# Graph attention with gathered neighbours: the norm constants made for four tiles at once, the output stores spaced, and four operations moved between engines

## The chip, the cores and the metric

The kernel runs on one core of a Trainium2 chip. A core has five engines that work side by side, each through its own list of instructions in order: TensorE (PE in the profile: matmuls; PEld is its loading of weights), VectorE (DVE), ScalarE (ACT), GpSimd (POOL) and SyncE (SP, which only starts DMA transfers here). An engine whose next instruction has to wait stands still, even if a later one could run. The metric is the time of one execution on the device in microseconds, the median of several runs. The profile is of one further execution.

## The reference

Sixteen graphs of 1024 nodes with 512 features share one adjacency matrix. Layer norm and a rectifier, projections to queries, keys and values with 8 heads of 64, softmax over the neighbours of each node, a weighted sum of their values, and x added at the end:

```python
h = jnp.maximum(_layernorm(x, axis=-1), 0.0)
q = (h @ Wq + bq).reshape(b, n, H, HD)      # k and v alike
scores = jnp.einsum('bihd,bjhd->bhij', q, k) / jnp.sqrt(jnp.float32(HD))
mask = jnp.where(adj == 0, jnp.float32(-1000000000.0), jnp.float32(0.0))
weights = jax.nn.softmax(scores + mask[None, None, :, :], axis=-1)
out = jnp.einsum('bhij,bjhd->bihd', weights, v)
x = x + out.reshape(b, n, H * HD)
```

The adjacency matrix is sparse: an entry is one with a probability that falls with the node's number, 1/256 on average, and the diagonal is one.

## The kernel before

The kernel sorts the nodes by degree, so that a tile of 128 nodes has rows of like length, and makes a list of each node's neighbours. That is the preparation, once for all graphs. For each graph it then loads x in sorted order, normalizes it, makes keys and values, stores them in DRAM, and gathers for every node the keys and values of its neighbours, one neighbour ("slot") of 128 nodes per indirect transfer. A tile has 2 to 11 slots, taken in "units" of at most four; the rows that are longer than 11 have the rest in unit 11 ("pieces"):

```python
CAPS = (11, 8, 6, 5, 4, 3, 3, 2)      # slots of tiles 0 to 7
UNITS = (                              # (tile, first slot, slots); the tile -1 is that of the pieces
    (7, 0, 2), (6, 0, 3), (5, 0, 3), (4, 0, 4), (3, 0, 3), (3, 3, 2), (2, 0, 3),
    (2, 3, 3), (1, 0, 4), (1, 4, 4), (0, 0, 4), (-1, 0, 4), (0, 4, 4), (0, 8, 3),
)                                      # units 0 to 13
POOL_FOLDS = (2, 3, 8, 9, 10, 11, 12)
BY_VECTOR = {2: 1, 3: 0, 4: 1}         # slots of a unit that VectorE weighs; ScalarE weighs the others
POOLS = dict(x=14, h=2, pht=2, hT=11, pkv=2, kvt=3, q=2, q0=1, g=6, acc=2, o=1)   # buffers
```

The order of every engine's instructions is worked out while the kernel is built. A plan lists the operations with an engine, a length, a place (the smaller, the earlier it is preferred), what they follow and which buffers they use; it then lets the five engines run on paper and notes what starts when. The kernel is emitted in just that order:

```python
add(("stats", n), "DVE", 0.90, p - ahead - 3.82, [("load_x", n)], [("x", n)])
if b and n % 2:
    add(("variance", n // 2), "DVE", 0.33, ..., [("stats", n - 1), ("stats", n)])
    add(("power", n // 2), "POOL", 0.82, ..., [("variance", n // 2)])
    add(("shift", n // 2), "DVE", 0.23, ..., [("power", n // 2)])
add(("norm", n), "ACT", 0.81, p - 6.37, [("shift", n // 2) if b else ("load_x", n)], [("x", n), ("h", n)], delay=0.09)
add(("flip", n), "PE", 0.62, p - 3.76, [("norm", n)], [("h", n), ("pht", n)])
add(("unflip", n), "ACT", 0.58, p - 1.28, [("flip", n)], [("pht", n), ("hT", n)])
# [...] proj_kv, evict_kv, store_kv (keys and values), queries (pq), gathers
add(("multiply", k), "DVE", 0.15 + 0.533 * count, i, slots + [q_of[q]], [g, q])
add(("score", k), "DVE", 0.15 + 0.533 * count, i - -0.31, [("multiply", k)], [g])
# [...] exponent, row_sums, share, weigh_v, weigh_s, fold, join, add_up, scale
add(("residual", b, home), "POOL", 1.42, i + 2.49, [("scale", b, home)], [o, ("x", n)])
add(("put_out", b, home), "POOL", 1.5, i + 0.07, [("residual", b, home)], [("x", n)], delay=4.0, moves=0.75)
```

What the operations do, as far as they matter here (cut):

```python
def stats(n):                                   # VectorE: mean and variance of a tile
    m, k = divmod(n, 2)
    nc.vector.bn_stats(st, X[n]); nc.vector.bn_aggr(MV[m][:, k, :], st)
def variance(m): nc.vector.tensor_scalar_add(RSTD[m], MV[m][:, :, 1], EPS)
def power(m):    nc.gpsimd.tensor_tensor(RSTD[m], RSTD[m], minus_half.to_broadcast([P, 2]), ALU.pow)
def shift(m):    nc.vector.scalar_tensor_tensor(SHIFT[m], MV.pop(m)[:, :, 0], -1.0, RSTD[m], op0=ALU.mult, op1=ALU.mult)
def norm(n):     nc.scalar.activation(HN[n], X[n], AF.Relu, bias=shift, scale=scale)
def flip(n):     # TensorE: four transposes of h into pht; unflip copies pht to hT on ScalarE
def multiply(i): nc.vector.tensor_tensor(k, k, Q[b, t][:, None, :].to_broadcast([P, count, D]), ALU.mult)   # gathered keys by pq
def score(i):    nc.vector.tensor_reduce(weights[:, w, :], heads(G[i][:, :count, 0, :]), AX.X, ALU.add)
def weigh_v(i):  # VectorE: the last n slots' values by their weights, one instruction
    n = by_vector(b, B, count)
def weigh_s(i, s):                              # ScalarE: one slot, one instruction per head
    for h in range(H):
        nc.scalar.activation(v[:, h, :], v[:, h, :], AF.Identity, scale=weights[:, c + s, h : h + 1])
def fold(i, first, n):                          # adds slots first to first+n on to slots 0 to n
    engine = nc.gpsimd if n == 1 and i % NU in POOL_FOLDS else nc.vector
    engine.tensor_tensor(v[:, 0:n], v[:, 0:n], v[:, first : first + n], ALU.add)
def residual(b, t):                             # x + attention
    (nc.vector if shares_in(b, B, t) and b == B - 1 else nc.gpsimd).tensor_tensor(rows, rows, add, ALU.add)
def put_out(b, t):                              # stores the rows at their nodes' places
    nc.gpsimd.indirect_dma_start(out=out_rows, out_offset=on(ap=perm[:, t : t + 1], axis=0), in_=..., in_offset=None, element_offset=b * N * D)
```

Units of four slots are folded twice: slots 2 and 3 on to 0 and 1 (VectorE), then 1 on to 0 (VectorE or, in the units of POOL_FOLDS, GpSimd). The sum of tile 0 over its units, with the pieces among them, is made on TensorE (add_up, into acc); those of the other tiles on VectorE (join). The last graph is taken in another order, with more of the sums on TensorE.

Of the kernel before, what the change touches and what calls it, by code (L numbers as in the profile page):

```python
# [32 lines left out]
P = 128  # L33
# [33 lines left out]
POOL_FOLDS = (2, 3, 8, 9, 10, 11, 12)  # L67
# [4 lines left out]
BY_VECTOR = {2: 1, 3: 0, 4: 1}  # L72
BY_VECTOR_LAST = {2: 1, 3: 1, 4: 2}
POOLS = dict(x=14, h=2, pht=2, hT=11, pkv=2, kvt=3, q=2, q0=1, g=6, acc=2, o=1)
# [95 lines left out]
def plan_of(B):  # L170
# [30 lines left out]
    for what, known, made in (("key", [("keys",)], -52.56), ("rank", [("ranks",)], -49.22)):  # L201
        for half in range(2):
            row = ("q", what, half)
            add(("flip_row", what, half), "PE", 0.6, made, known, [row])
            add(("copy_row", what, half), ("DVE", "ACT")[half], 0.65, made, [("flip_row", what, half)], [row, sources])
    rows = lambda what: [("copy_row", what, half) for half in range(2)]
    for t in range(NT):
        add(("rank_of", t), ("DVE", "ACT")[t >= NT // 2], 1.25, (-47.51, -44.58)[t >= NT // 2], rows("key"))
    add(("ranks",), "DVE", 1.4, -47, [("rank_of", t) for t in range(NT)])
    add(("ends",), "DVE", 0.7, -45, rows("rank"), [sources])  # L210
    for t in range(NT):
        add(("list_of", t), "DVE", 2.5, -35.55 + t, [("ends",), ("no_diagonal", t)], [sources])
        behind = lambda name: [(name, t - 2)] if t > 1 else [("zeros",)]
        add(("tell", t), "POOL", 1.3, -35.76 + 0.3 * t, [("ranks",), ("shift", (t - NT) // 2)] + behind("tell"), delay=2.0)
        add(("spread", t), "POOL", 1.3, -28.64 + t, [("list_of", t)] + behind("spread"), delay=2.0)
    add(("collect", "told"), "SP", 0.05, -39, [("tell", t) for t in range(NT)], delay=2.6)
    add(("collect", "lists"), "SP", 0.05, -31, [("spread", t) for t in range(NT)], delay=2.6)
    add(("others",), "DVE", 1.3, -34.38, [("ends",)], [sources])
    add(("perm_of",), "DVE", 0.5, -31, [("collect", "told")])
    add(("spots",), "DVE", 3.9, -38.36, [("collect", "lists")])  # L220
    add(("long_rows",), "POOL", 1.3, -39.76, [("perm_of",)], [("g", -2)], 2.5, 1.5)
    add(("long_blocks", 0), "DVE", 1.25, -18.02, [("long_rows",), ("others",)], [sources, ("g", -2)])
    for k in range(1, 5):
        add(("long_blocks", k), "DVE", 2.0, -32.13 + 0.1 * k, [("long_blocks", k - 1)], [("g", -2)])
# [4 lines left out]
    add(("count_pieces",), "DVE", 0.9, 2.64, [("longest", ROUNDS - 1)])  # L229
# [6 lines left out]
    add(("slots", 0), "DVE", 2.0, 3.84, [("pieces",), ("spots",)])  # L236

    for n in range(-NT, tiles):
        b, j = divmod(n, NT)
        ahead = 0 if n >= 0 else 11.19 - 1.3 * j  # L240
        p = (b - 1) * NU + j * rate if b > 0 else j * rate - 19.58 if b == 0 else 1.5 * j - 44.63
        if n >= 0:
            known = [("perm_of",)] if b == 0 else []
            add(("load_x", n), "POOL", 1.40, p - 7.17, known, [("x", n)], delay=4.5, moves=0.75)
        if b:
            add(("stats", n), "DVE", 0.90, p - ahead - 3.82, [("load_x", n)], [("x", n)])
        if b and n % 2:
            add(("variance", n // 2), "DVE", 0.33, p - ahead - 5.75, [("stats", n - 1), ("stats", n)])
            add(("power", n // 2), "POOL", 0.82, p - ahead - 4.87, [("variance", n // 2)])
            add(("shift", n // 2), "DVE", 0.23, p - ahead - 4.31, [("power", n // 2)])  # L250
        add(("norm", n), "ACT", 0.81, p - 6.37, [("shift", n // 2) if b else ("load_x", n)], [("x", n), ("h", n)], delay=0.09)
        add(("flip", n), "PE", 0.62, p - 3.76, [("norm", n)], [("h", n), ("pht", n)])
        add(("unflip", n), "ACT", 0.58, p - 1.28, [("flip", n)], [("pht", n), ("hT", n)])
        if b == 0:
            continue
        for w in range(2):
            e = p - 0.39 + 0.3 * w
            ready = [("unflip", n)]
            if n < 0:
                ready += [("round", "kv"[w], 2), ("load_w", "kv"[w])]  # L260
            add(("proj_kv", n, w), "PE", 3.70, e, ready, [("hT", n), ("pkv", n, w)])
            add(("evict_kv", n, w), "ACT", 0.58, e - 0.43, [("proj_kv", n, w)], [("pkv", n, w), ("kvt", n)])
        ready = [("evict_kv", n, w) for w in range(2)]
        if n >= 0:
            add(("store_kv", n), "SP", 0.1, p, ready, [("kvt", n)], delay=2.5, moves=1.5)
        else:
            add(("store_kv", n), "POOL", 1.35, p, ready + [("ranks",)] + ([("store_kv", n - 1)] if n > -NT else []), [("kvt", n)], delay=2.5, moves=1.5)

    q_of = {}
    for k in range(units):  # L270
        b, u = divmod(k, NU)
        i = b * NU + (LAST_ORDER.index(u) if b == B - 1 else u)
# [3 lines left out]
        if q not in q_of:  # L276
            p = i - 2.15
            if t >= 0:
                ready = [("unflip", n)] + ([("round", "q", 2), ("load_w", "q")] if b == 0 else [])
                add(("queries", b, t), "PE", 3.66, p, ready, [("hT", n), q])  # L280
                if t == 0:
                    add(("copy_q", b), "ACT", 0.57, p + 0.5, [("queries", b, 0)], [q, ("q0", b)])
            else:
                add(("queries", b, t), "PE", 0.9, p, [("copy_q", b)], [q, ("q0", b)])
            q_of[q] = ("queries", b, t)
# [3 lines left out]
        for s, slot in enumerate(slots):  # L289
            if is_own(u, s):  # L290
                add(slot, "SP", 0.1, i - -0.51, stored if b == 0 else [("store_kv", n)], [g], delay=2.5, moves=1.5)
                continue
            add(slot, "POOL", 1.35, i - 4.33 + 0.1 * s, stored, [g], delay=4.0, moves=1.5)
        vector = by_vector(b, B, count)
        add(("multiply", k), "DVE", 0.15 + 0.533 * count, i, slots + [q_of[q]], [g, q])
        add(("score", k), "DVE", 0.15 + 0.533 * count, i - -0.31, [("multiply", k)], [g])
        shares = shares_in(b, B, t)
        add(("exponent", k), "ACT", 0.22, i + -0.73, [("score", k)], delay=0.60)
        weights = ("exponent", k)
        if shares:  # L300
            weights = ("share", k)
            add(("row_sums", b, t), "DVE", 0.47, i + 0.98, [("exponent", k)])
            add(weights, "DVE", 0.3, i + -1.42, [("row_sums", b, t)])
        weighed = []
        if vector:
            weighed.append(("weigh_v", k))
            add(("weigh_v", k), "DVE", 0.15 + 0.533 * vector, i + 1.76, [weights], [g])
        for s in range(count - vector):
            weighed.append(("weigh_s", k, s))
            add(("weigh_s", k, s), "ACT", 1.97, i + 0.86 + 0.1 * s, [weights], [g], delay=0.20)  # L310
        for n in folds(b, B, t, count):
            on_pool = n[1] == 1 and u in POOL_FOLDS
            add(("fold", k, *n), "POOL" if on_pool else "DVE", 1.38 if on_pool else 0.84 * n[1] - 0.15, i + 0.78, weighed, [g], delay=1.79 if on_pool else 0.15)
# [4 lines left out]
        if without_tensor(b, B, home):  # L318
            acc = ("g", b * NU + parts[0])
            added = weighed  # L320
            if u != parts[0]:
                added = [("join", k)]
                add(("join", k), "DVE", 0.84, i + 2.33, weighed + summed, [g, acc])
            summed = added
        else:
            add(("add_up", k), "PE", 0.88 * (1 if folds(b, B, t, count) else count), i + 0.84, weighed + ([("add_up", k - 1)] if u != parts[0] else []), [g, acc])
            added = [("add_up", b * NU + v) for v in parts]
        if u == parts[-1]:
            n = b * NT + NT - 1 - home
            if shares:  # L330
                add(("residual", b, home), "POOL" if b < B - 1 else "DVE", 1.42, i + 5.31, weighed, [g, ("x", n)])
                add(("put_out", b, home), "POOL", 1.5, i + 2.40, [("residual", b, home)], [("x", n)], delay=4.0, moves=0.75)
                continue
# [3 lines left out]
            if home == 0:  # L337
                pieces = [b * NU + v for v in parts if UNITS[v][0] < 0]
                add(("more", b), "DVE", 0.22, pieces[0] + 1.35, [("exponent", v) for v in pieces])
                add(("pass_on", b), "PE", 0.3, pieces[0] + 0.69, [("more", b)], [("acc", b, "more")])  # L340
                exps.append(("pass_on", b))
            add(sums, "DVE", 0.47 if home else 0.72, i + 1.79, exps, [] if home else [("acc", b, "more")])
            add(("scale", b, home), "DVE", 0.85, i + 0.78, [sums] + added, [acc, o])
            add(("residual", b, home), "POOL", 1.42, i + 2.49, [("scale", b, home)], [o, ("x", n)])
            add(("put_out", b, home), "POOL", 1.5, i + 0.07, [("residual", b, home)], [("x", n)], delay=4.0, moves=0.75)
    return plan.ordered(POOLS)

# [16 lines left out]
def by_vector(b, B, count):  # L364

    return (BY_VECTOR if b < B - 1 else BY_VECTOR_LAST)[count]

# [14 lines left out]
def main_path(tc, x, adj, Wq, bq, Wk, bk, Wv, bv, out, sums, cover):  # L382
# [10 lines left out]
    with ExitStack() as ctx:  # L393
# [200 lines left out]
        def stats(n):  # L594
            m, k = divmod(n, 2)
            st = small.tile([P, nc.vector.BN_STATS_DIM], F32, tag="st", name=f"st_{n}")
            if m not in MV:
                MV[m] = small.tile([P, 2, nc.vector.BN_AGGR_DIM], F32, tag="mv", name=f"mv_{m}")
# [3 lines left out]
        def made(m, at, name):  # L602
            t = 2 * m + NT
            return before["told"][:, t : t + 2, at] if m < 0 else small.tile([P, 2], F32, tag=name, name=f"{name}_{m}")
# [5 lines left out]
        def power(m):  # L610
            nc.gpsimd.tensor_tensor(RSTD[m], RSTD[m], minus_half.to_broadcast([P, 2]), ALU.pow)
# [5 lines left out]
        def norm(n):  # L617
            b, t = tile_at(n)
            m, k = divmod(n, 2)
# [271 lines left out]
        def weigh_v(i):  # L891
            b, t, w, c, count = unit(i)
            n = by_vector(b, B, count)
# [69 lines left out]
        def residual(b, t):  # L963
            rows = X[b * NT + NT - 1 - t]
            add = G.pop(b * NU + parts_of(t)[0])[:, 0, 1, :] if shares_in(b, B, t) else O.pop((b, t))
            (nc.vector if shares_in(b, B, t) and b == B - 1 else nc.gpsimd).tensor_tensor(rows, rows, add, ALU.add)  # L966
# [202 lines left out]
```

## Time and profile before

| | |
|---|---|
| median of 3 runs | 1759.28 us (1757.06 to 1759.89) |
| span of the profiled execution | 1752.1 us |
| TensorE, VectorE, ScalarE, GpSimd busy | 1618.9, 1558.5, 1489.1, 1330.9 us |
| TensorE clock granted, mean | 0.97 |
| moved by DMA | 531.73 MB, 303 GB/s |
| indirect gathers / loads of x / output stores on GpSimd | 608 / 128 / 128 |
| shift, 60 of 128x2 | 52.6 us, 877 ns each |
| power, 60 of 128x2 | 60.6 us, 1010 ns each |
| folds of 128x512: GpSimd / VectorE | 120 of 1279 ns / 181 of 823 ns |
| residuals on GpSimd | 127 of 1268 to 1288 ns |
| weighing of 128x512 on VectorE | 128 of 828 ns |

A line of the profile that tells of waits reads: who waited, at which line of the kernel, for whom; then the total in us, how often, and the longest. A line of the timeline reads: start, length, engine, line, operation, what is written from what, and in brackets how long the engine stood before it, and what released it. GpSimd's transfers are told as DMA_INDIRECT: the time is that in which GpSimd writes their descriptors, not that of the transfer.

### The profile page before, as it was taken

How to read it: one execution, taken by the hardware profiler on the slowest of the kernel's cores; microseconds unless marked ns; L12 is line 12 of the kernel's file. 1: busy time of each engine (PE TensorE's matmuls, PEld its weight loads, DVE VectorE, ACT ScalarE, POOL GpSimd, SP SyncE). 2: the span in 40 equal slices, each digit the busy share in tenths (PEclk: the TensorE clock that was granted, in tenths of full speed). 3: DMA queues.
4: the chain of work that ended last, by engine and by line, in shares of the span. 5: the costliest groups of instructions: out<-in, count | busy, mean ns of one | idle time of the engine just before them, and what ended most of it. 6: DMA issues, size and time to landing. Idle time of an engine off the chain costs nothing.

```text
span 1752.1 us, 19712 instructions
## 1 busy us (share of the span) xinstructions
PE 1618.9 (92%) x4295; PEld 751.8 (43%) x4295; DVE 1558.5 (89%) x1922; ACT 1489.1 (85%) x5556; POOL 1330.9 (76%) x1235
## 2 busy tenths in 40 slices
PE   6979898999999999999999999999999999999796
PEld 3444444444444444444444444444444444444333
DVE  5788989899898979989898998989989898988897
ACT  5359989898898988889898888989899898889965
POOL 4757778787787868877787877878787787877774
PEclk9989999999999999999999999999999999999989
DMA  5388889888898988988898888989988898888894
GB/s 219 132 321 293 309 292 344 309 324 316 287 329 304 339 298 309 323 284 327 305 350 303 304 304 293 346 318 328 322 294 313 293 346 304 318 311 290 310 359 169
DMA packets 150742, 531.73 MB, mean 303 GB/s; under 512 B 19916, under 2 KB 19916, under 8 KB 150616
## 3 DMA queue, kind: packets, MB, share of 16 engines
q0 software_dynamic: 109840, 390.70, 62.5%
q1 hardware_dynamic: 40776, 139.71, 21.7%
q8 instruction: 36, 0.59, 0.1%
q14 instruction: 90, 0.74, 0.1%
HBM read 429.51 MB, written 100.82 MB: 303 GB/s over the span
## 4 chain that ended last, share of the span: by engine, by line
PE 45%; DVE 18%; POOL 8%; ACT 6%; issue 4%; DMA 3%; POOLq 0%; DVEq 0%
PE pq L642 15%; PE pk L642 12%; PE pv L642 8%; DVE g L876 5%; ACT g L902 4%; PE acc L925 4%; DVE g L907 3%; DVE weights L880 3%; PE pht L632 3%; POOL g L866 3%; DVE shift L615 3%; DMA out_dram<-x,perm 2%; POOL x L966 2%; POOL g L907 1%; DVE g L896 1%
## 5 line engine op out<-in xcount | busy, mean ns | idle before, releaser
L902 ACT ACTIVATE g<-g,weights 128x64 f32<-128x64 f32 x4768 | 1180.3, 340 | 3.2 <-DVE weights L889 2.2
L866 POOL DMA_INDIRECT g<-kv,index x608 | 626.1, 1030 | 204.6 <-issue 143.5
L876 DVE TENSOR_TENSOR g<-g,pq 128x1536 f32<-128x1536 f32 (+2 forms) x208 | 389.1, 1872 | 95.4 <-PE pq L642 90.9
L642 PE MATMUL pq<-wq,hT 128*128 128x512 f32 x1024 | 460.3, 592 | 0.0
L642 PE MATMUL pk<-wk,hT 128*128 128x512 f32 x960 | 439.0, 601 | 1.8 <-ACT hT L637 1.7
L642 PE MATMUL pv<-wv,hT 128*128 128x512 f32 x960 | 431.6, 592 | 0.0
L880 DVE TENSOR_REDUCE weights<-g 128x32 f32<-128x2048 f32 (+2 forms) x224 | 423.2, 1890 | 0.6
L907 DVE TENSOR_TENSOR g<-g 128x512 f32<-128x512 f32 (+1 forms) x271 | 281.1, 1038 | 21.9 <-ACT g L902 19.8
L642 PEld LDWEIGHTS pq<-wq,hT 128*128 128x128 f32 x1024 | 194.7, 190 | 228.0 <-issue 224.7
L642 PEld LDWEIGHTS pk<-wk,hT 128*128 128x128 f32 x960 | 185.8, 194 | 212.9 <-issue 206.0
L642 PEld LDWEIGHTS pv<-wv,hT 128*128 128x128 f32 x960 | 182.5, 190 | 205.3 <-issue 201.9
L969 POOL DMA_INDIRECT out_dram<-x,perm x128 | 148.1, 1157 | 79.2 <-DMA out_dram<-x,perm 34.2
L625 ACT ACTIVATE h<-x,shift,rstd 128x512 f32<-128x512 f32 x120 | 91.3, 809 | 91.5 <-DVE shift L615 91.5
L590 POOL DMA_INDIRECT x<-in_x_dram,perm x128 | 135.9, 1062 | 34.9 <-issue 32.4
L907 POOL TENSOR_TENSOR g<-g 128x512 f32<-128x512 f32 x120 | 153.5, 1279 | 10.7 <-DVE g L907 7.2
L632 PE MATMUL pht<-ident,h 128*128 128x128 f32 x512 | 86.2, 308 | 80.2 <-ACT h L625 78.2
L632 PEld LDWEIGHTS pht<-ident,h 128*128 128x128 f32 x512 | 68.3, 158 | 139.5 <-ACT h L625 104.5
L896 DVE TENSOR_TENSOR g<-g,weights 128x512 f32<-128x512 f32 (+1 forms) x134 | 114.5, 855 | 2.2 <-ACT weights L884 1.7
L653 ACT COPY kvt<-pv 128x512 f32<-128x512 f32 x120 | 69.2, 577 | 43.0 <-PE pv L642 43.0
L966 POOL TENSOR_TENSOR x<-x,o 128x512 f32<-128x512 f32 x67 | 86.3, 1288 | 25.0 <-DVE o L957 22.1
L925 PE MATMUL acc<-g,ident 128*128 128x512 f32 x170 | 95.6, 682 | 2.8 <-POOL g L907 2.8
L637 ACT COPY hT<-pht 128x512 f32<-128x512 f32 x128 | 72.1, 575 | 26.9 <-PE pht L632 26.9
(231 smaller groups left out, 1187.0 us busy)
## 6 DMA issues: line engine op xcount, KB each, us to landing
g<-kv SPq DMA_DIRECT2D x128, 512.0 KB
kv<-kvt SPq DMA_DIRECT2D x120, 512.0 KB
g<-kv,index POOLq DMA_INDIRECT x608, 7.2
adj<-in_adj_dram SPq DMA_DIRECT2D x8, 512.0 KB
x_first<-in_x_dram SPq DMA_DIRECT2D x8, 256.0 KB
x<-in_x_dram,perm POOLq DMA_INDIRECT x128, 4.6
out_dram<-x,perm POOLq DMA_INDIRECT x128, 5.0
wk<-in_L_gnn_Wk_dram SPq DMA_DIRECT2D x1, 1024.0 KB
```

The costliest lines, as they stand in the source:

```text
L590: nc.gpsimd.indirect_dma_start(out=X[n][:], out_offset=None, in_=x_rows, in_offset=on(ap=perm[:, t : t + 1], axis=0), element_offset=b * N * D
L632: nc.tensor.transpose(PH[n][:, c, :], hn[:, ts(c, P)], ident)
L642: nc.tensor.matmul(pt, HT[n][:, c, :], W[name][:, c, :], start=False, stop=(c == DC - 1))
L866: nc.gpsimd.indirect_dma_start(out=G[i][:, s].rearrange("p j d -> p (j d)"), out_offset=None, in_=KV[b % len(KV)][:], in_offset=on(ap=inde ...
L876: nc.vector.tensor_tensor(k, k, Q[b, t][:, None, :].to_broadcast([P, count, D]), ALU.mult)
L880: nc.vector.tensor_reduce(weights[:, w, :], heads(G[i][:, :count, 0, :]), AX.X, ALU.add)
L896: nc.vector.tensor_tensor(v, v, own.to_broadcast([P, n, H, HD]), ALU.mult)
L902: nc.scalar.activation(v[:, h, :], v[:, h, :], AF.Identity, scale=weights[:, c + s, h : h + 1])
L907: engine.tensor_tensor(v[:, 0:n], v[:, 0:n], v[:, first : first + n], ALU.add)
L925: nc.tensor.matmul(ACC[b, home], owner_t if t < 0 else ident, v[:, s, :], start=(u == parts_of(home)[0] and s == 0), stop=(u == parts_of(h ...
L966: (nc.vector if shares_in(b, B, t) and b == B - 1 else nc.gpsimd).tensor_tensor(rows, rows, add, ALU.add)
L969: nc.gpsimd.indirect_dma_start(out=out_rows, out_offset=on(ap=perm[:, t : t + 1], axis=0), in_=X.pop(b * NT + NT - 1 - t)[:], in_offset=No ...
```

## The change

Four parts, and an order that is worked out anew:

- The norm's constants (variance, power, shift) are made for four tiles in one instruction each, not for two. The tiles of the first pass (which prepares the first graph) stay in pairs.
- Each output store follows, in the plan, the landing of the one before it. The stores write to one DRAM tensor at places known only at run time, so the kernel waits for that in any case; now the plan knows of it and can put other work between.
- Two of GpSimd's folds (units 10 and 12) and the sum with x of tile 4 go to VectorE; in the last graph, tile 7's sum with x goes from VectorE to GpSimd.
- VectorE weighs one slot of unit 6, which ScalarE did.

Beside these, lengths and places in the plan are set anew. All this is for taking load off GpSimd and ScalarE and for fewer hand-overs between engines ahead of the normalization. Nothing is computed differently.

```diff
-POOL_FOLDS = (2, 3, 8, 9, 10, 11, 12)
+POOL_FOLDS = (2, 3, 8, 9, 11)
+ONE_MORE = (6,)
+VECTOR_RESIDUAL = (4,)
 [...]  places and lengths of the preparation
-        if b and n % 2:
-            add(("variance", n // 2), "DVE", 0.33, p - ahead - 5.75, [("stats", n - 1), ("stats", n)])
-            add(("power", n // 2), "POOL", 0.82, p - ahead - 4.87, [("variance", n // 2)])
-            add(("shift", n // 2), "DVE", 0.23, p - ahead - 4.31, [("power", n // 2)])
-        add(("norm", n), "ACT", 0.81, p - 6.37, [("shift", n // 2) if b else ("load_x", n)], [("x", n), ("h", n)], delay=0.09)
-        add(("flip", n), "PE", 0.62, p - 3.76, [("norm", n)], [("h", n), ("pht", n)])
-        add(("unflip", n), "ACT", 0.58, p - 1.28, [("flip", n)], [("pht", n), ("hT", n)])
+        m, k, size = group_of(n)
+        if b and k == size - 1:
+            add(("variance", m), "DVE", 0.33, p - ahead - 5.41, [("stats", n - k) for k in range(size)])
+            add(("power", m), "POOL", 1.1, p - ahead - 4.87, [("variance", m)])
+            add(("shift", m), "DVE", 0.37, p - ahead - 4.52, [("power", m)])
+        add(("norm", n), "ACT", 0.76, p - 6.38, [("shift", m) if b else ("load_x", n)], [("x", n), ("h", n)], delay=0.02)
+        add(("flip", n), "PE", 0.62, p - 3.85, [("norm", n)], [("h", n), ("pht", n)])
+        add(("unflip", n), "ACT", 0.53, p - 2.19, [("flip", n)], [("pht", n), ("hT", n)])
 [...]
-            add(slot, "POOL", 1.35, i - 4.33 + 0.1 * s, stored, [g], delay=4.0, moves=1.5)
-        vector = by_vector(b, B, count)
+            add(slot, "POOL", 1.35, i - 1.86 + 0.1 * s, stored, [g], delay=4.0, moves=1.5)
+        vector = by_vector(b, B, u)
 [...]  lengths and places of multiply to add_up
-            add(("residual", b, home), "POOL", 1.42, i + 2.49, [("scale", b, home)], [o, ("x", n)])
-            add(("put_out", b, home), "POOL", 1.5, i + 0.07, [("residual", b, home)], [("x", n)], delay=4.0, moves=0.75)
+            add(("residual", b, home), *by, i + 3.48, [("scale", b, home)], [o, ("x", n)])
+            add(("put_out", b, home), "POOL", 1.35, i + 0.07, [("residual", b, home)] + one_by_one, [("x", n)], delay=4.0, moves=0.75)
+            one_by_one = [("put_out", b, home)]
 [...]
+def group_of(n):
+    size = 4 if n >= 0 else 2
+    return n // size, n % size, size
 [...]
+    return BY_VECTOR[count] + (u in ONE_MORE) if b < B - 1 else BY_VECTOR_LAST[count]
+def residual_by_vector(b, B, t):
+    return t in VECTOR_RESIDUAL and (b < B - 1 or t in LAST_DIRECT)
 [...]
-            nc.gpsimd.tensor_tensor(RSTD[m], RSTD[m], minus_half.to_broadcast([P, 2]), ALU.pow)
+            nc.gpsimd.tensor_tensor(RSTD[m], RSTD[m], minus_half.to_broadcast([P, 2 if m < 0 else 4]), ALU.pow)
 [...]
-            (nc.vector if shares_in(b, B, t) and b == B - 1 else nc.gpsimd).tensor_tensor(rows, rows, add, ALU.add)
+            (nc.vector if residual_by_vector(b, B, t) else nc.gpsimd).tensor_tensor(rows, rows, add, ALU.add)
```

## The prediction

> **What bounds the kernel now.** I read the page first, for the shares of the engines:
>
> ```profile
> PE 1618.9 (92%) x4295; PEld 751.8 (43%) x4295; DVE 1558.5 (89%) x1922; ACT 1489.1 (85%) x5556; POOL 1330.9 (76%) x1235
> PE 45%; DVE 18%; POOL 8%; ACT 6%; issue 4%; DMA 3%; POOLq 0%; DVEq 0%
> ```
>
> Four engines are nearly full at once, and the chain of waits (second line) passes through all of them: no engine sets the end alone. So I need the length of one graph in the steady part, and what each engine does without in it. The instruction that adds up the weights of the long rows' pieces ("more", VectorE) runs once per graph; the timeline has it at 302.85 us for the second graph and at 1548.79 us for the fourteenth: 12 graphs in 1245.9 us, 103.8 us each. Before the second lies the preparation, after the fourteenth some 200 us with the last graph, which takes another order. The waits of just these 12 graphs, longest first:
>
> ```profile
> DVE g L876 <- PE pq L642: 73.6, 41, 4.1
> ACT h L625 <- DVE shift L615: 71.3, 36, 5.0
> PE pht L632 <- ACT h L625: 68.1, 24, 4.0
> ...
> ACT kvt L653 <- PE pv L642: 34.6, 36, 1.9
> POOL out_dram L969 <- DMA out_dram<-x,perm: 28.8, 9, 4.3
> ```
>
> The columns are us in total, times, longest. TensorE waits 68.1 / 12 = 5.7 us per graph for normalized rows (h); ScalarE, which makes them, 5.9 us for VectorE's shift; VectorE 6.1 us for queries of TensorE (pq). This is a ring. TensorE's own work is less than it looks: in the timeline one projection (bias and eight matmuls) starts every 3.65 us (720.27, 723.92, 727.57); 24 of them make 87.6, eight tiles of transposes at 0.44 make 3.5, four sums into PSUM at 0.86 make 3.4, pieces 1.0: 95.5 us of 103.8. The gap of 8.3 us is what the change can win. VectorE is busy 94 us of such a graph, ScalarE 93, GpSimd 81, DMA 0.88 of it (the view by stages).
>
> Two places show how the ring loses time. GpSimd, in order of time (start, us):
>
> ```profile
> 745.30 1.01 POOL L969 DMA_INDIRECT out_dram<-x,perm  x1 [0.17 <-POOL x L966]
> 746.61 0.97 POOL L866 DMA_INDIRECT g<-kv,index  x1 [0.31 <-issue]
> 747.88 0.94 POOL L866 DMA_INDIRECT g<-kv,index  x1 [0.30 <-issue]
> 752.55 1.00 POOL L969 DMA_INDIRECT out_dram<-x,perm  x1 [3.73 <-DMA out_dram<-x,perm]
> ```
>
> Two output stores with only two gathers between: the second stands 3.73 us until the first has landed, and all gathers behind it stand too. And VectorE:
>
> ```profile
> 756.76 1.75 DVE L876 TENSOR_TENSOR g<-g,pq 128x1536 f32<-128x1536 f32 x1 [4.13 <-PE pq L642]
> ...
> 762.09 2.60 DVE L907 TENSOR_TENSOR g<-g 128x1024 f32<-128x1024 f32 x1
> ...
> 766.36 2.44 DVE L615 SCALAR_TENSOR_TENSOR shift<-mv,rstd 128x2 f32<-128x2 f32 x1 [0.54 <-POOL rstd L611]
> ```
>
> A shift of 128x2 takes 2.44 us (the shortest take 0.14), a fold of 128x1024 2.60 (elsewhere 1.22): each lies beside GpSimd's additions. The transposes behind that shift begin at 769.70 after 2.03 us of waiting.
>
> **What the Trainium skill says.** "SBUF — State Buffer", section "Who interferes with whom": VectorE and GpSimd share a port pair under an exclusive lock, and a VectorE instruction with two SBUF inputs stands against a GpSimd instruction that reads SBUF, for its whole length. The trace agrees: shift, fold and weighing (two SBUF inputs) are stretched, while the multiply by pq (one input in PSUM, 2.28 us) and the score reduction (2.27 us) are not. "DMA: Bandwidth & Descriptors", section "Anatomy of one DMA — SWDGE (gpsimd) path": a wait on a semaphore happens on the issuing sequencer, before dispatch. The 3.73 us above are that; a store lands 5.0 us after issue (median). "Perfetto Trace Analysis", section "Identifying the Most-Contended Engine": matmul busy time isn't a good measure of TensorE's headroom. Here the 1176.8 busy of 1245 us (94.5%) hides waits: one projection in the trace is shown with 5.29 us instead of 3.60.
>
> **The change, part by part (per ordinary graph; 15 of 16 are).**
> 1. Norm constants by four tiles: two groups instead of four. VectorE loses two variances (0.26 us) and two shifts (0.96 us, mean of the steady part): -2.4. GpSimd loses two powers: -2.1. The built order shows more: before, after 44 of 64 powers a fold or residual of GpSimd follows at once and takes the lock just as the shift wants to run; in the changed order a gather follows each of the 30 group powers, which reads no such tile. So the two remaining shifts should go from 0.96 to 0.15: -1.6.
> 2. Two folds (units 10 and 12) to VectorE: +2 x 0.75 there (0.68 free, 0.82 mean), -2 x 1.28 on GpSimd.
> 3. One residual (tile 4) to VectorE: +0.73 (as the join of that form), -1.27 on GpSimd. In the last graph tile 7's goes the other way, into the tail: +0.5 us once.
> 4. One slot of unit 6 from ScalarE to VectorE: +0.8 there; -2.0 on ScalarE (eight activations, 2.04 us in the timeline).
> 5. Stores spaced: same instructions. By the GpSimd order and 1.25 us per gather (0.94 busy and 0.30 between two in the rows above), the nearest pair of an ordinary graph goes from 3.5 us to 4.8 us, against 5.0 to land. So the wait mostly shrinks, from 28.8 / 12 = 2.4 us per graph to about 0.5.
> GpSimd's additions and powers fall from 24.5 to 18.6 us. The other two-input work on VectorE is stretched by 4.5 us per graph (row of folds 181 x 0.14 and 90 x 0.25, weighing 128 x 0.15, over 15); a quarter less is -1.1. Sums: VectorE -4.0 +1.5 +0.7 +0.8 -1.1 = -2.1; ScalarE -2.0; GpSimd -5.9; TensorE 0. No engine gets fuller, and TensorE's 95.5 stays: the gain must come out of its gap.
> 6. The order. Walking both orders by hand with the durations above: before, TensorE puts the first transposes after one projection and three queries, and the query of tile 3 behind two further projections; the walk has VectorE wait 4 us there, as the trace does. After, three queries and three sums come first, then the transposes. VectorE's work from one shift to the next is about 46.5 and 48.5 us, TensorE's between the two groups of transposes 49.2 and 46.3. These balance; I find one wait of VectorE for pq, 2 us at unit 6, and 3 to 4 us of slack elsewhere. That walk gives 97 to 98 us per graph.
>
> A walk has no landing times, no DMA at 0.88 (0.88 x 103.8 / 98 = 0.93) and no ScalarE at 91 of 98. I add 3 us for them: 100.8, thus 3.0 less per graph; over 14 intervals -42. The preparation is reordered (the first multiply goes ahead of the pieces, two more statistics ahead of it), as is the tail; I take 0 for both, +-5, and 3 us back for disturbances. 1759 - 42 + 3 = 1720.
>
> **Rivals.** (a) Bunching: four tiles must have landed before the first may be normalized, so x is read earlier and TensorE waits longer but twice instead of four times. For it: the wait for the shift is already the second longest, and the x load of the last tile of a group waits for a store to free its buffer. Against: statistics wait for loads 0.3 us in the 12 graphs. It would leave 103 to 104: 1750 to 1765. (b) VectorE becomes the bound: it takes four more large instructions, each open to the lock. If the shifts stay stretched (1.6) and the others are stretched by 0.2 each, it is +0.3 instead of -2.1, and the gain halves: 1738. (c) Gathers or DMA: at 0.88 share, waits for g<-kv are small now (4.1 us in all), but with a shorter graph they grow and take the place of the pq waits: 102, 1735. (d) Everything meets: the ring closes at 97.5 and 14 x 6 = 88 us go: 1675.
>
> **Range and chances.** I weigh the balance of part 6 with the rivals: 1720, 8 in 10 between 1692 and 1752. Two per cent is at 1724, near the middle: faster 0.53, within 2% 0.43, slower 0.04; for slower, bunching would have to cost more than all wins.
>
> **What would show it.** Shift's mean from 0.88 to under 0.3 (part 1); TensorE's wait for h from 5.7 to about 2 to 3 us per graph and VectorE's for pq from 6.1 to about 2 to 3 (part 6); GpSimd's wait for stores under 1 (part 5); VectorE's busy time lower by about 30 us, GpSimd's by 80 to 90, ScalarE's by 30; graphs at 101 us. I am wrong if the two waits only change places (a), if VectorE's busy time rises (b), or if gathers head the list (c).

## The result, and the profile after

| | before | changed |
|---|---|---|
| median | 1759.07 us | 1732.09 us (1729.5 to 1734.44) |
| span of the profiled execution | 1752.1 us | 1732.7 us |
| one graph in the steady part | 103.8 us | 101.5 us |

The ratio is 0.9848, with a 95% interval of 0.9828 to 0.9868: 1.5% faster. (The profiled execution of the kernel before happened to be 5 us faster than its timed median, so the two traces differ by 19.4 us where the medians differ by 27.) The runs were made on several chips, on which the kernel before took 1757 to 1807 us; every ratio below is to the kernel before, or to the changed kernel where that is said, on the same chip.

The page of the changed kernel, the engines and the chain of waits:

```profile
PE 1599.7 (92%) x4262; PEld 741.7 (43%) x4295; DVE 1510.7 (87%) x1921; ACT 1468.5 (85%) x5436; POOL 1264.7 (73%) x1161
...
PE 76%; DMA 8%; DVE 2%; ACT 2%; issue 2%; POOL 1%; POOLq 0%; DVEq 0%
PE pk L663 23%; PE pv L663 23%; PE pq L663 20%; DMA g<-kv,index 6%; PE acc L946 3%; DMA kv<-kvt 2%; PE pht L653 2%; DVE g L897 2%; PE pv L661 1%; PE pq L661 1%; PE pk L661 1%; POOL g L887 1%; ACT hT L658 0%; ACT h L646 0%; ACT q L878 0%
```

Every engine is busy for less time, TensorE with the same matmuls too (1618.9 us before; more of this below). The chain, which went through all four engines with TensorE at 45%, now stays on TensorE for 76% of the span and leaves it for transfers: gathers (g<-kv) and stores of keys and values (kv<-kvt), where VectorE had 18% before. The waits in the steady part of the changed kernel (300 to 1520 us, 12 graphs; total, times, longest):

```profile
DVE g L897 <- DMA g<-kv,index: 61.8, 33, 4.2
...
PE pq L661 <- DVE g L897: 43.1, 22, 4.0
...
POOL g L887 <- DMA kv<-kvt: 39.2, 12, 4.4
...
POOL out_dram L990 <- DMA out_dram<-x,perm: 9.4, 8, 2.8
...
DVE g L897 <- PE pq L663: 8.1, 6, 2.8
...
ACT h L646 <- DVE shift L636: 6.3, 14, 0.5
```

The waits that headed the list before are nearly gone: VectorE for queries from 6.1 to 0.7 us per graph, ScalarE for the shift from 5.9 to 0.5, GpSimd for stores from 2.4 to 0.8; TensorE's wait for h, 5.7 before, isn't among the answer's rows at all. Three new ones stand in their place, each absent or small before: gathers 5.1 us per graph, the store of keys and values 3.3 (12 times, so once per graph), and TensorE waiting for VectorE's multiply 3.6.

These three are one chain, at the change from one graph to the next. In the timeline of the changed kernel, TensorE:

```profile
1521.19 3.60 PE L663 MATMUL pv<-wv,hT 128*128 128x512 f32 x8
1524.63 1.02 PE L946 MATMUL acc<-g,ident 128*128 128x512 f32 x2
1525.48 0.28 PE L963 MATMUL p_more<-more,owner_t 128*128 128x8 f32 x2
...
1533.78 1.02 PE L946 MATMUL acc<-g,ident 128*128 128x512 f32 x2
1538.47 0.59 PE L661 MATMUL pq<-bq_parts,chosen 128*128 128x512 bf16 x1 [3.67 <-DVE g L897]
1538.85 4.94 PE L663 MATMUL pq<-wq,hT 128*128 128x512 f32 x8
```

GpSimd in the same stretch:

```profile
1531.39 1.98 POOL L887 DMA_INDIRECT g<-kv,index  x1 [3.92 <-DMA kv<-kvt]
```

And VectorE:

```profile
1537.19 1.22 DVE L897 TENSOR_TENSOR g<-g,pq 128x1024 f32<-128x1024 f32 x1 [3.95 <-DMA g<-kv,index]
```

Read it in order: the last value projection of the next graph ends at about 1524.8; its copy and store have to land before that graph's first gather may be issued (1531.39); the gather lands at about 1537; the first multiply runs, and when it is done it frees one of the two PSUM buffers of queries, for which TensorE has waited 3.67 us.

The last TensorE row shows that such a wait costs more than its length. Its eight matmuls take 4.94 us, where those of the first row take 3.60: the trace has the granted TensorE clock at 0.50 from 1539 to 1541 us. Between 300 and 1540 us a stretch at 0.50 follows each of TensorE's six waits of 3.2 to 4.0 us, and none of its waits of 1.5 to 1.9; the trace of before has 14 such stretches there. The mean clock over the span went from 0.970 to 0.981. As an estimate, (1 - 0.970) x 1752.1 = 53 us and (1 - 0.981) x 1732.7 = 33 us went to the slow clock, 20 us less, though not all of that lies on the chain. So part of the gain comes by way of the clock. That the waits cause the slow stretches is inferred from their order in time.

The two kinds of shift (shortest, median and longest in ns), first before:

```profile
L615 DVE SCALAR_TENSOR_TENSOR shift<-mv,rstd x60: 143/154/2447, 105.0 to 1626.5; 128x2 f32<-128x2 f32 x60
```

and changed:

```profile
L636 DVE SCALAR_TENSOR_TENSOR shift<-mv,rstd x30: 153/155/204, 112.9 to 1590.8; 128x4 f32<-128x4 f32 x30
```

Twice as many tiles in the same 155 ns, and none is stretched any more.

### The profile page after: what moved, and what is told of

Its sections match the earlier page's. It is cut to its first block, busy times and chain, and to the rows that moved or that the text cites. A ratio compares the mean times of both kernels' runs of the same rounds, so it can differ in the third digit from the quotient of the medians.

```text
span 1732.7 us, 19484 instructions
## 1 busy us (share of the span) xinstructions
PE 1599.7 (92%) x4262; PEld 741.7 (43%) x4295; DVE 1510.7 (87%) x1921; ACT 1468.5 (85%) x5436; POOL 1264.7 (73%) x1161
## 4 chain that ended last, share of the span: by engine, by line
PE 76%; DMA 8%; DVE 2%; ACT 2%; issue 2%; POOL 1%; POOLq 0%; DVEq 0%
PE pk L663 23%; PE pv L663 23%; PE pq L663 20%; DMA g<-kv,index 6%; PE acc L946 3%; DMA kv<-kvt 2%; PE pht L653 2%; DVE g L897 2%; PE pv L661 1%; PE pq L661 1%; PE pk L661 1%; POOL g L887 1%; ACT hT L658 0%; ACT h L646 0%; ACT q L878 0%
## 5 line engine op out<-in xcount | busy, mean ns | idle before, releaser
L923 ACT ACTIVATE g<-g,weights 128x64 f32<-128x64 f32 x4648 | 1144.2, 338 | 13.8 <-DVE weights L910 12.8
L663 PE MATMUL pq<-wq,hT 128*128 128x512 f32 x1024 | 473.8, 607 | 0.1
L928 DVE TENSOR_TENSOR g<-g 128x512 f32<-128x512 f32 (+1 forms) x301 | 260.0, 868 | 23.2 <-ACT g L923 22.9
L990 POOL DMA_INDIRECT out_dram<-x,perm x128 | 136.9, 1069 | 52.5 <-issue 19.8
L928 POOL TENSOR_TENSOR g<-g 128x512 f32<-128x512 f32 x90 | 117.2, 1302 | 71.3 <-DVE g L928 62.3
L917 DVE TENSOR_TENSOR g<-g,weights 128x512 f32<-128x512 f32 (+1 forms) x149 | 129.3, 868 | 2.3 <-ACT weights L905 2.2
L905 ACT ACTIVATE weights<-weights 128x32 f32<-128x32 f32 (+2 forms) x224 | 49.7, 222 | 85.8 <-DVE weights L901 85.5
L646 ACT ACTIVATE h<-x,shift,rstd 128x512 f32<-128x512 f32 x120 | 94.5, 811 | 31.5 <-issue 19.4
L661 PE MATMUL pq<-bq_parts,chosen 128*128 128x512 bf16 x126 | 49.1, 390 | 52.4 <-DVE g L897 52.4
L946 PE MATMUL acc<-g,ident 128*128 128x512 f32 x170 | 85.6, 617 | 12.3 <-issue 6.9
L653 PE MATMUL pht<-ident,h 128*128 128x128 f32 x512 | 73.5, 276 | 18.2 <-ACT hT L658 16.5
```

The source lines that it names most:

```text
L653: nc.tensor.transpose(PH[n][:, c, :], hn[:, ts(c, P)], ident)
L661: nc.tensor.matmul(pt, chosen, bias[name], start=True, stop=False)
L663: nc.tensor.matmul(pt, HT[n][:, c, :], W[name][:, c, :], start=False, stop=(c == DC - 1))
L917: nc.vector.tensor_tensor(v, v, own.to_broadcast([P, n, H, HD]), ALU.mult)
L946: nc.tensor.matmul(ACC[b, home], owner_t if t < 0 else ident, v[:, s, :], start=(u == parts_of(home)[0] and s == 0), stop=(u == parts_of(h ...
```

## The experiments

My theory after this reading had two halves. What was won came from the new order, not from the loads moved or the instructions saved. What was missed is the ring at the graph's end (last projection, store, gather, multiply, query buffer). The rivals: the loads carry the gain; or gathers land late merely because the DMA engines are 0.89 busy.

### The ring at the graph's end

Gathers read the table of graph 0, written in the preparation, and stores of later graphs go to two other tables, so no gather waits for its own graph's store. The output is then another one. Transfers, instructions and every engine's order stay.

```diff
-                in_=KV[b % len(KV)][:],
+                in_=KV[0][:],
-            kv = KV[b % len(KV)]
+            kv = KV[0] if n < 0 else KV[1 + b % 2]
```

On the changed kernel:

> The changed kernel, every engine's order unchanged, but all gathers and own-slot loads read the keys and values of graph 0, written in the preparation, and later graphs' stores go to two other tables: no gather waits for a store of its own graph (the output is then another one). Theory A (the ring at the graph's end: last projection, store, gather, first multiply, free query buffer on TensorE): TensorE's waits for VectorE's multiply (43 us in 12 graphs) and GpSimd's for the store (39 us) go, a graph takes 97 us instead of 101.6, in all 1665 to 1685. Theory B (gathers land late because the DMA engines are 0.89 busy): the multiplies still wait for gathers some 5 us per graph, 1715 to 1732.

Measured: 1706.69 us, 0.9513 (0.9491 to 0.9534) of the kernel before. (The expected times are for the first chip; there 0.9513 would be 1673 us.) That chip had no run of the changed kernel, so it was done again beside one:

> The changed kernel beside the next three on one chip: 0.965 to 0.987 of the kernel before (0.985 and 0.970 were measured on two chips).

> The changed kernel with its order, gathers from graph 0's table (the output is then another one), now beside the changed kernel on one chip. By the ring at the graph's end, a graph is 3 us shorter, in all 0.972 to 0.980 of the changed kernel. If the difference of the first such run came from the chip, 0.99 to 1.00.

Measured: the changed kernel 1726.64 us, 0.9837 (0.9818 to 0.9856); with the ring cut 1685.03 us, 0.9590 (0.9573 to 0.9606). That is 0.976 of the changed kernel, 41.6 us; a graph takes 98.3 us, not 101.0. Its waits in 300 to 1500 us:

```profile
POOL g L928 <- DVE g L928: 42.1, 25, 2.9
...
DVE g L897 <- DMA g<-kv,index: 13.3, 17, 2.4
```

The longest is now GpSimd's for VectorE's folds, which is off the chain (TensorE has 69% of it). The gathers' wait fell from 57.2 us (the changed kernel on this chip) to 13.3, though the same bytes move in a shorter time; so it was not the DMA engines' load that made them late. Nor do quicker reads from one table explain it: a gather lands 6.7 us after its issue (median), 6.9 in the changed kernel. TensorE's wait for a query buffer, 40.4 us there, went as well (1.1 us are left); in the timeline the third query now follows 9.6 us after the pieces' sums are passed on, where it was 13.0 in the rows above. No wait of TensorE is longer than 1.1 us between 300 and 1500 us, and its clock stays at 1.00 there. The ring is shown, and it costs 2.4%.

The same edit on the kernel before:

> The same edit on the kernel before (gathers read graph 0's keys and values; the output is then another one). In its trace neither GpSimd nor the multiplies wait for the store at the graph's end, so theory A expects next to nothing: 1745 to 1760. If the edit helps in another way (less waiting for SyncE's own-slot loads, say), both kernels gain alike and the run on the changed kernel proves nothing of the ring.

Measured: 1794.31 us, 0.9997 (0.9982 to 1.0012): nothing, as the ring expects. It didn't bind before; the change uncovered it.

### Order or loads

The engine moves were taken back in two ways. First through the plan, which then works out an order for them:

```diff
-POOL_FOLDS = (2, 3, 8, 9, 11)
-ONE_MORE = (6,)
-VECTOR_RESIDUAL = (4,)
+POOL_FOLDS = (2, 3, 8, 9, 10, 11, 12)
+ONE_MORE = ()
+VECTOR_RESIDUAL = ()
```

> The changed kernel with the two folds and tile 4's sum with x back on GpSimd and unit 6's slot back on ScalarE. If the loads count for little (no engine but TensorE on the chain), 1728 to 1742. If taking load from GpSimd and ScalarE was what helped, 1745 to 1765, with ScalarE's or GpSimd's waits heading the list.

Measured: 1869.92 us, 1.0431 (1.0402 to 1.0461), a graph 110 us. That looked like a verdict for the loads. Among its longest waits, whole span:

```profile
DVE g L928 <- ACT g L923: 89.9, 49, 7.5
DVE g L897 <- DMA g<-kv,index: 84.0, 36, 7.2
PE pht L653 <- ACT h L646: 80.0, 14, 11.2
```

The first is VectorE's wait for slots that ScalarE weighs, the work that was given back, and speaks for the loads; the other two, for gathers and for h, can as well come from the order. Loads and order changed together here, so this run can't part them. So the same was done with the order of the changed kernel kept, and only the engine changed where an operation is emitted; and, as the mark, the changed kernel beside it:

```diff
-            engine = nc.gpsimd if n == 1 and i % NU in POOL_FOLDS else nc.vector
+            engine = nc.gpsimd if n == 1 and i % NU in POOL_FOLDS + (10, 12) and i // NU < B - 1 else nc.vector
-            (nc.vector if residual_by_vector(b, B, t) else nc.gpsimd).tensor_tensor(rows, rows, add, ALU.add)
+            nc.gpsimd.tensor_tensor(rows, rows, add, ALU.add)
 [...]  in weigh_v, for unit 6: weigh_s(i, count - 1) instead
```

> The changed kernel itself, beside the others on one chip: 0.983 to 0.987 of the kernel before, as in the first measurement. It is the mark for what follows.

> The changed kernel with every engine's order as it is, but the two folds, tile 4's sum with x and unit 6's slot on the engines of before, each at the place in the list where it stands now. If the order carries the gain and the loads little, 1.00 to 1.015 of the changed kernel (GpSimd +3.8 us, ScalarE +2.0, VectorE -2.7 per graph; none of them on the chain). If the loads carry it, 1.03 or more, as in the run in which the plan worked out a new order for the old loads (1.043 of before).

Measured: the changed kernel 1752.1 us, 0.9704 (0.9641 to 0.9767), below the expected span on this chip; with the old engines in its order 1758.53 us, 0.9721 (0.9662 to 0.9779). The difference, 6 us of 1752 (0.2% by the ratios, 0.4% by the medians), is within the intervals. The trace of the latter, whole span:

```profile
PE acc L949 <- POOL g L931: 39.1, 15, 3.4
...
DVE g L897 <- DMA g<-kv,index: 21.7, 21, 1.8
...
PE pq L661 <- DVE g L897: 3.2, 4, 1.1
```

TensorE now waits 39.1 us for GpSimd's folds and only 3.2 for a query buffer: it is held up elsewhere in the graph, and the ring, it seems, then has its slack. One wait took another's place.

The counterpart is the kernel before in its own order with the operations on the changed kernel's engines (same manner of edit, other way round):

> The kernel before with its own order, the two folds and tile 4's sum with x on VectorE and one slot of unit 6 too, each at the place in the list where it stood. If loads count for little in either order, 0.99 to 1.005 of the kernel before. If they are what the change lives from, 0.975 to 0.985.

Measured: 1782.16 us, 1.0133 (1.0111 to 1.0154). I had expected nothing; it is slower, a graph 105.8 us. Its waits in 300 to 1500 us:

```profile
PEld pht L632 <- ACT h L625: 104.0, 31, 6.1
ACT h L625 <- DVE shift L615: 98.5, 44, 5.4
PE pht L632 <- ACT h L625: 83.0, 23, 5.3
DVE g L876 <- PE pq L642: 68.3, 46, 4.1
```

In the order of before, VectorE's work stands ahead of the shift for which TensorE waits: more work there, and TensorE's wait for h grows from 67.6 (the kernel before, same stretch) to 83.0 us. So, with both orders held: the moves alone cost 1.3%, and within the new order they are worth 0.2 to 0.4%, which isn't clear of noise. The order is worth 2.8% with the old loads (0.9721, one chip) and 2.9% with the new ones (1.0133 to 0.9837, another chip). The gain is the order's.

### The groups of four

> The changed kernel with norm constants by two tiles as before, all places and the engine moves kept. If the groups of four took away TensorE's waits for h (5.7 us per graph before, 0.1 after), these come back: 1745 to 1760 and over 3 us of waits for h per graph. If the new order did it, 1725 to 1740 with few waits for h. The built order puts transposes and two projections of the next graph ahead of the first queries, so there is little of the wait for the query buffer either way.

```diff
-    size = 4 if n >= 0 else 2
+    size = 2
```

Measured: 1776.42 us, 0.9900 (0.9866 to 0.9934), a graph 103.8 us. The ratio lies higher than the changed kernel's on other chips (0.970 to 0.985; it was not run on this one), but not for the reason expected: TensorE waits only 8.8 us for h in the whole span. It stands 51.2 us before its sums (acc), VectorE waits 39.9 us for queries and GpSimd 52.2 us for ScalarE's exponents instead. The plan's order had changed here too, so once more with the order kept and the constants of a group made by two instructions instead of one:

```diff
+            for h in range(0, 2 if m < 0 else 4, 2):
-            nc.gpsimd.tensor_tensor(RSTD[m], RSTD[m], minus_half.to_broadcast([P, 2 if m < 0 else 4]), ALU.pow)
+                nc.gpsimd.tensor_tensor(RSTD[m][:, h : h + 2], RSTD[m][:, h : h + 2], minus_half.to_broadcast([P, 2]), ALU.pow)
 [...]  variance and shift alike
```

> The changed kernel with its order, but variance, power and shift of each group of four made by two instructions of two tiles each, one after the other at the same place. The number of these instructions is then that of before, and only their place is that of the group. VectorE +0.5 us per graph, GpSimd +2; if the instructions saved were worth anything, 1.01; if it is the place and the hand-overs, 1.000 to 1.004.

Measured: 1750.28 us, 0.9662 (0.9598 to 0.9726), 0.999 of the changed kernel: the instructions saved are worth nothing that shows. All 60 shifts of 128x2 take 156 ns in the mean here, so it was the new order, not their number, that took away their stretching. What is left for a group of four to give is its place, two hand-overs per graph instead of four. Whether an order tuned for pairs could do as well wasn't tried.

### The spacing of the stores

```diff
-            add(("put_out", b, home), "POOL", 1.35, i + 0.07, [("residual", b, home)] + one_by_one, ...)
+            add(("put_out", b, home), "POOL", 1.35, i + 0.07, [("residual", b, home)], ...)
```

> The changed kernel with the stores' order left free in the plan (they still wait for one another on the chip). If the spacing matters, GpSimd's waits for stores go from 9 us in 12 graphs back to about 29, and the time to 1.005 to 1.015 of the changed kernel. If not, 1.00.

Measured: 1798.13 us, 0.9950 (0.9928 to 0.9972), which is 1.026 of the changed kernel, a larger loss than expected. But GpSimd's wait for stores is 16.0 us in the whole span, against 16.3 in the changed kernel on that chip. The loss is not that of waiting for stores; the plan made another order, in which a graph takes 104.1 us. What the spacing by itself is worth stays open: no run changed it alone.

### A new set of places

The operations of the changed kernel, with the plan's places set anew (and some of them by tile and unit):

> The changed kernel with the same operations and only the plan's places set anew, so that the keys and values of the last tiles of a graph come a little earlier on TensorE and the stores are spaced wider; the preparation is reordered too. Three queries still come ahead of the next transposes, so the wait for a free query buffer stays. If order alone is worth per cents, 0.985 to 0.995 of the changed kernel; if what is left is the ring alone, 0.995 to 1.005.

```diff
+BUMP = {('flip', 4): -3.01, ('stats', 0): -2.82, ...}      # [...] added to the place of an operation of a tile or unit
+        turn = phase(key)
+        if turn:
+            place = place + BUMP.get(turn, 0)
```

Measured: 1730.12 us, 0.9863 (0.9839 to 0.9887), the same as the changed kernel's 0.9837 on that chip within the intervals; a graph 101.1 us against 101.0. In 300 to 1500 us:

```profile
POOL x L995 <- DVE o L986: 52.2, 12, 4.3
...
POOL out_dram L998 <- DMA out_dram<-x,perm: 34.4, 10, 4.5
DVE g L905 <- PE pq L671: 33.4, 18, 3.0
...
DVE g L905 <- DMA g<-kv,index: 25.6, 24, 3.0
```

The gathers' wait was halved (25.6 us from 57.2), the query buffer's fell to 10.7 us, and the time stayed: GpSimd's waits for VectorE's scaling (o) and for stores and VectorE's for queries came instead, and TensorE now stands 24.6 us before its sums (acc). The ring isn't removed by moving places within these buffers, at least not by this set. None of the kernels in which each graph gathers its own keys and values beat the changed one beyond the intervals.

## Why the prediction held, and where its steps did not

The time, 1732, lies in the range, 12 us above the point. By its steps:

- **The bound** was read rightly: nothing but TensorE's gap could be won. The gap fell from 8.3 to 6.0 us per graph. One reading in it is wrong: the projection of 5.29 us hides no wait, but ran at a granted clock of 0.50 (772 to 774 us). The gap of 8.3 us is 5.7 of waits for h and, as an estimate, 2.1 of slow clock ((1 - 0.98) x 103.8, with the mean clock of these graphs); that of 6.0 is 3.6 for a query buffer, 1.0 for the copied transposes (hT) and about 1.0 of clock ((1 - 0.99) x 101.5).
- **Part 1**: shifts at 0.158 us in the mean, as predicted. But the run with pairs in the same order shows that saving these instructions is worth nothing in time that is clear of noise: VectorE isn't on the chain.
- **Parts 2 to 4, the sums of load**: VectorE fell by 47.8 us, more than the 30 that I named, because its folds are less stretched (128x512 from 823 to 697 ns, 128x1024 from 1470 to 1267: the row takes 260.0 us instead of 281.1, with 30 folds more). GpSimd fell by 66 where I said 80 to 90, in part because a power for four tiles takes more than one for two (1.22 against 1.01 us in the mean). ScalarE fell by 21 where I said 30. Right in sign; and as the fixed orders show, not what made the gain.
- **Part 5**: the wait for stores under 1 us per graph, as predicted (0.8).
- **Part 6, the order**: h and pq were to fall to 2 to 3 us per graph; they fell to almost nothing (h) and 0.7 (pq). Here the prediction was too careful. It erred the other way in the next point, so that the time came within 12 us is in part luck. The rival of bunching (a) is refuted by the same numbers, and (b) by VectorE's fall. In (d), 14 x 6 makes 84, not 88; its 1675 goes with the 84.
- **The term that was mis-sized**: "A walk has no landing times ... I add 3 us for them". The walk gave 97 to 98 us per graph; with the ring cut a graph takes 98.3, so the walk agrees with a kernel without it. The rest came to not 3 us but 3.5 to 4.5 over the walk, 2.7 of them in one place that I could have seen: GpSimd's first gather waits for the graph's last store, and the walk took gathers as there. Rival (c) had the symptom (102 us, 1735), and its sign of being wrong came: gathers head the list (61.8 us). But it put them down to the DMA share, and that is refuted.
- **Preparation and tail**, taken as 0 +-5: by a mark on TensorE (the passing on of the pieces' sums) the first graph's comes 1.8 us later than before, the fourteenth's 25.0 earlier, the fifteenth's 21.8, and the end 19.4. So start and tail lost about 1.8 and 2.4, and one graph before the last 3.1. VectorE's mark tells it otherwise, 6.3 us earlier in the first graph, because VectorE now runs ahead of TensorE. With a ring it matters on which engine one sets the mark; it is the one on which the chain lies.

## What to carry to other kernels

In this kernel, where several engines are nearly full and wait for each other in a ring, removing instructions or moving load was worth little by itself; what counted was the order. A wait of TensorE can cost more than its length, so look at the granted clock behind it. To judge an edit in a kernel whose order is computed, run it also with the order held fixed: here the two answers were 1.043 and 0.972. And in walking through an order by hand, carry the landing times across the borders of loop passes: the wait that replaced all others was a store that the next pass reads.

## What the runs showed of the hardware

How much one kernel differs between chips: the one before took 1757, 1793 and 1807 us (medians beside the three sets of runs), and the changed kernel's ratio was 0.9837 to 0.9848 where the kernel before took 1757 to 1759 us, but 0.9704 where it took 1807. The mean granted TensorE clock of the kernel before was 0.969, 0.962 and 0.960 in these three sets; which is cause and which effect isn't shown. This gain of a few per cent is a number for one chip. GpSimd's power takes 1.05 us for 128x4 and 0.74 for 128x2 before (medians; 1.22 and 1.01 in the mean), so four tiles cost less than twice what two did.
